# Last batch element of a two-layer graph kernel: s_i and s_j from two-column products right behind the transposes, and the maxima over its first half of keys during its own attention

## The chip, the cores and the metric

The kernel runs on one core of one Trainium2 chip. The metric is the device time of one execution in microseconds, as the median over several runs. A profiled execution gives the times of single instructions; its span runs from the first to the last instruction.

## The reference

Inputs are x (8 batch elements, 2048 nodes, 256 features, float32) and an adjacency matrix of 2048 x 2048. Two layers follow each other:

```python
# layer 0: attention with 4 heads of 64, keys in 8 chunks of 256, a softmax inside each chunk
scores = clip(q @ k.T / 8, -10, 10);  scores = where(mask == 0, -10, scores)
ctx = sum over chunks of softmax(scores in the chunk) @ v in the chunk
h = layernorm(x + (layernorm(ctx @ Wo.T + bo + x) * gamma + beta))
# layer 1: graph attention
Wh = h @ W;  s_i = Wh @ a1;  s_j = Wh @ a2
e = leaky_relu(s_i[:, None] + s_j[None, :], 0.2), -inf where there is no edge
out = layernorm(h + elu(softmax(e) @ Wh))
```

Since the leaky ReLU rises monotonically, the largest e of a query is leaky_relu(s_i + the largest s_j among its neighbours). Layer 1 subtracts it before the exponential, so it needs, for each query, a maximum over all neighbouring keys.

## The kernel before

**Beats.** The nodes are cut into 4 query blocks of 512 (`ib`) and 16 key chunks of 128 (`c`). Layer 0 goes through batch elements, blocks and chunks in one program of 512 beats, one key chunk of one block in each: the scores of four heads on TensorE (L899), the cap by the mask on VectorE (two L909), the exponential on ScalarE (L912), and the products with v of the chunk pair before (L928), copied by ScalarE (L936, L942). Sums of a pair go through two small DMAs and a reciprocal (dc, L950, rd, r), and VectorE and GpSimd scale and add them (L963, L964). Even beats carry the dc and rd DMAs. Batch element 7, the last, has beats 448 to 511. Then come beats without layer 0, here called the tail.

**The order of the work is written out by hand.** Each engine executes its instructions in the order in which the program issues them, and so does SP, the queue that issues all DMAs. Generators are advanced one step per beat in `end_beat`: before beat 512 those of `ahead`, then those of `fins`; from beat 512 on the other way round. A step waits on its engine if its input isn't there, and everything behind it on that engine waits too.

**fin(b, ib)** ends layer 0 for a block: output products (`po`, L357), adds, statistics (L316, L317), a power on GpSimd (L322), scaling on ScalarE (L329), gamma and beta, statistics and scaling once more, the store of h, and eight transposes of h (L383) that ScalarE copies into `hT` (L384). `hT` is stored to DRAM, except that of the last block of batch element 7. Each stage is a step of its own beat. For block (7,3), fin's steps lie in the tail, the transposes in beat 520.

**Layer 1** runs one batch element behind, in steps of one key chunk: ScalarE's L714, VectorE's L718 (with s_j as a scalar) and L723 (the mask), the exponential L727, sums on GpSimd (L734, L736), products with Wh (L746, for the last batch element L761). In the tail one step starts per beat: at its beginning the last block of batch element 6, (6,3), remains, then come the four blocks of batch element 7.

**prelude(b)** prepares layer 1 of batch elements 0 to 6: it loads hT, multiplies it with `W_aug` (L398; 258 columns, that is W with W·a1 and W·a2 as two more), takes the columns s_j, 0.2 s_j and s_i out of `wh` into `sj` (`key_columns`, L408 to L410), transposes s_j and sends it through DRAM to a row on all partitions (`key_rows`, L416 to L421), and then goes over all queries: `half_max` (L438) adds the row to a half row of `far`, which is 0 at edges and hugely negative elsewhere, and keeps the maximum. Half rows come through the two buffers `fb`, loaded by SP (L430) as they get free. `less_max` (L453 to L457) and `query_rows` make what layer 1 needs for a block (`ab`).

**last_prelude(7)** does this for batch element 7. In beats 500, 504 and 508 it loads hT of blocks 0 to 2, and two beats after each it computes `wh` of the block, in the place of kT, which attention has read by then, and its columns of `sj`. From beat 511 it takes the maxima over the first half of the keys (16 of them, `half(it, 0)`), one per beat up to beat 512 and two after. In beat 514 it issues loads of the second half rows of `far`, 4 MB, into eight buffers. When hT of block (7,3) is there it computes `wh` and `sj` of that block and the second row, and takes the maxima over the second half.

Matmul results of all these helpers share two PSUM buffers, tag "m" in the pool `ps_m`; a helper's matmul waits until the buffer's last reader is through.

Of the kernel before, what the change touches and what calls it, by code (L numbers as in the profile page):

```python
# [9 lines left out]
F32 = mybir.dt.float32  # L10
# [9 lines left out]
P = 128  # L20
CLIP = 10.0
EPS = 1e-5
SLOPE = 0.2
# [5 lines left out]
def tile_adj_attention__then__gat(  # L29
# [35 lines left out]
    nc = tc.nc  # L65
    B, N, F = x.shape
    H, D = 4, 64
    CHUNK = 256
    KC = F // P
    NT = N // P  # L70
    IB = 512
    NIB = N // IB
    TPB = IB // P
# [4 lines left out]
    HN = N // 2  # L78
# [259 lines left out]
    fin_near = [0] * B  # L338
# [3 lines left out]
    def fin(b, ib, ctxT):  # L342


        xt = one.tile([P, TPB, F], F32, tag="x", name=f"x{b}_{ib}")
        nc.sync.dma_start(out=xt, in_=x[b, ts(ib, IB), :].rearrange("(t p) f -> p t f", p=P))
        yield
        y = one.tile([P, TPB, F], F32, tag="y", name=f"y{b}_{ib}")
        nc.gpsimd.tensor_add(y, xt, bc_rows(bo_bc))  # L349
        nc.gpsimd.tensor_add(xt, xt, bc_rows(beta_bc))  # L350
        while (b, ib) not in ctx_done or ctx_done[b, ib] == beat:
            yield
        for t2 in range(TPB // 2):
            po = ps_m.tile([P, 2, F], F32, tag="m", name=f"po{b}_{ib}_{t2}")
            for j in range(2):
                for k in range(KC):
                    nc.tensor.matmul(  # L357
                        po[:, j, :],
                        ctxT[:, k, ts(2 * t2 + j, P)],
                        WT["o"][:, k, :],  # L360
                        start=(k == 0),
                        stop=(k == KC - 1),
                    )
            nc.vector.tensor_add(y[:, ts(t2, 2), :], po, y[:, ts(t2, 2), :])
        mv, rstd = yield from stats(y, f"a{b}_{ib}")
        yield
        normalize(y, mv, rstd, f"a{b}_{ib}")
        yield
        engine = nc.vector if (b, ib) == (B - 1, NIB - 1) else nc.gpsimd
        engine.tensor_mul(y, y, bc_rows(gamma_bc))  # L370
        engine.tensor_add(y, y, xt)
        yield
        mv, rstd = yield from stats(y, f"b{b}_{ib}")
        yield
        normalize(y, mv, rstd, f"b{b}_{ib}")
        nc.sync.dma_start(out=h_d[b, ib], in_=y)
        fin_near[b] += 1
        yield
        hT = four.tile([P, KC, IB], F32, tag="xT", name=f"hT{b}_{ib}")
        for k in range(KC):  # L380
            pt = ps_m.tile([P, TPB, P], F32, tag="m", name=f"pt{b}_{ib}_{k}")
            for t in range(TPB):
                nc.tensor.transpose(pt[:, t, :], y[:, t, ts(k, P)], ident)  # L383
            nc.scalar.copy(hT[:, k, :], pt.rearrange("p t c -> p (t c)"))  # L384
        if (b, ib) == (B - 1, NIB - 1):
            states[b]["hT"] = hT
        else:
            nc.sync.dma_start(out=hT_d[b, ib], in_=hT)
# [12 lines left out]
    def load_hT(b, ib):  # L401
        t = four.tile([P, KC, IB], F32, tag="xT", name=f"hTl{b}_{ib}")
        nc.sync.dma_start(out=t, in_=hT_d[b, ib])
        return t

    def key_columns(wh, sj, r):

        nc.vector.tensor_copy(sj[:, 0, r], wh[:, :, F + 1])  # L408
        nc.vector.tensor_scalar_mul(sj[:, 1, r], wh[:, :, F + 1], SLOPE)
        nc.vector.tensor_copy(sj[:, 2, r], wh[:, :, F])  # L410

    def key_rows(b, sj, row, r):

# [61 lines left out]
    def prelude(b):  # L475


        st = states[b]
        while fin_near[b] < NIB:
            yield  # L480
        hts = [load_hT(b, ib) for ib in range(2)]
        yield
        yield
        while blocks_done < b * NIB:
            yield
        wh = one.tile([P, NT, F + 2], F32, tag="wh", name=f"wh{b}")
        for ib in range(NIB):
            wh_block(b, wh[:, ts(ib, TPB), :], hts[ib], ib)
            if len(hts) < NIB:
                hts.append(load_hT(b, len(hts)))  # L490
            yield
        sj = two.tile([P, 3, NT], F32, tag="sj", name=f"sj{b}")
        key_columns(wh, sj, slice(0, NT))
        yield
        sj_row = one.tile([P, N], F32, tag="sj_row", name=f"sj_row{b}")
        key_rows(b, sj, sj_row, slice(0, NT))
        st["wh"], st["sj"] = [wh[:, ts(ib, TPB), :] for ib in range(NIB)], sj
        fbs, fb_load = far_loads(b, [(it, hf) for it in range(NT) for hf in range(2)])
        yield
        yield  # L500
        for ib in range(NIB):
            m2 = two.tile([P, 2, TPB], F32, tag="m2", name=f"m2{b}_{ib}")
            for n in range(2 * TPB):
                half_max(sj_row[:, ts(n % 2, HN)], fbs.pop(0), m2[:, n % 2, n // 2 : n // 2 + 1])
                fb_load()
                if ib or n % 2:
                    yield
            less_max(sj, ib, m2, f"{b}_{ib}")
            yield
            ab_d = query_rows(m2, f"{b}_{ib}")  # L510
            yield

            while blocks_done < b * NIB + ib - 1:
                yield
            st["ab"][ib] = (beat + 2, query_bc(ab_d, f"{b}_{ib}"))

    def last_prelude(b):

        st = states[b]
        wh, rows = [None] * NIB, [None] * 2
        halves = [slice(0, HT), slice(HT, NT)]
        sj = None
        for ib in range(NIB - 1):

            while fin_near[b] <= ib or beat < 2 * total - 12 + 4 * ib:
                yield
            ht = load_hT(b, ib)
            yield  # L530
            yield
            wh[ib] = one.tile([P, TPB, F + 2], F32, tag=f"kT{ib}", name=f"wh{b}_{ib}")
            wh_block(b, wh[ib], ht, ib)
            if sj is None:
                sj = two.tile([P, 3, NT], F32, tag="sj", name=f"sj{b}")
            key_columns(wh[ib], sj, slice(ib * TPB, (ib + 1) * TPB))
            nc.vector.memset(wh[ib][:, :, F : F + 1], 1.0)
            yield
            if ib == 1:
                rows[0] = one.tile([P, HN], F32, tag="v0", name=f"sj_row{b}_0")  # L540
                key_rows(b, sj, rows[0], halves[0])
                fbs, fb_load = far_loads(b, [(it, 0) for it in range(NT)])
        m2 = one.tile([P, NIB, 2, TPB], F32, tag="m2l", name=f"m2{b}")
        firsts = list(range(NT))
        held = None

        def half(it, hf):
            fb = fbs.pop(0) if hf == 0 else held[it // 2][:, ts(it % 2, HN)]
            half_max(rows[hf], fb, m2[:, it // TPB, hf, it % TPB : it % TPB + 1])
            if hf == 0:  # L550
                fb_load()

        while "hT" not in st:
            for it in firsts[: 2 if beat > 2 * total else 1]:
                half(it, 0)
                firsts.remove(it)

            if beat >= 2 * total + 2 and held is None:
                held = []
                for n in range(HT):  # L560
                    fr = eight.tile([P, 2, HN], BF16, tag="e", name=f"far{b}_{n}")
                    nc.sync.dma_start(out=fr, in_=far[2 * n : 2 * n + 2, 1].rearrange("t p w -> p t w"))
                    held.append(fr.rearrange("p t w -> p (t w)"))
            yield
        wh[-1] = one.tile([P, TPB, F + 2], F32, tag=f"kT{NIB - 1}", name=f"wh{b}_{NIB - 1}")
        wh_block(b, wh[-1], st["hT"], NIB - 1)
        key_columns(wh[-1], sj, slice(NT - TPB, NT))
        nc.vector.memset(wh[-1][:, :, F : F + 1], 1.0)
        rows[1] = one.tile([P, HN], F32, tag="v1", name=f"sj_row{b}_1")
        key_rows(b, sj, rows[1], halves[1])  # L570
        st["wh"], st["sj"] = wh, sj
        yield
        while firsts:
            half(firsts.pop(0), 0)
        for ib in range(NIB):
            for t in range(TPB):
                half(ib * TPB + t, 1)
                if ib:
                    yield
            less_max(sj, ib, m2[:, ib], f"{b}_{ib}")  # L580
            ab_d = query_rows(m2[:, ib], f"{b}_{ib}")
            yield

            while blocks_done < b * NIB + ib - 1:
                yield
            st["ab"][ib] = (beat + 1, query_bc(ab_d, f"{b}_{ib}"))
# [213 lines left out]

    l1 = layer1()
    l1_live = True
    ahead = [prelude(b) for b in range(B - 1)] + [last_prelude(B - 1)]
    lows, edged, weighted = [], [], []
    agenda = {}
    beat = 0
# [228 lines left out]
```

## Time and profile before

| | us |
|---|---|
| median of 3 runs | 4392.35 |
| lowest and highest run | 4391.38, 4404.53 |
| the profiled execution, its own time | 4387.29 |
| its span, first to last instruction | 4385.5 |
| TensorE (PE) busy | 4064.2 (93%) |
| VectorE (DVE) busy | 3417.7 (78%) |
| ScalarE (ACT) busy | 2564.4 (58%) |
| GpSimd (POOL) busy | 1760.5 (40%) |

In the profile, PE is TensorE's matmuls and PEld its weight loads. A float32 matmul call appears as several instructions. The number in square brackets at the end of a row of the timeline is the engine's idle time ahead of it, and what released it. The chain view follows the work that ended last back from the end: at each step to what released it, or to the instruction before it on its engine.

### The profile page before, as it was taken

How to read it: one execution, taken by the hardware profiler on the slowest of the kernel's cores; microseconds unless marked ns; L12 is line 12 of the kernel's file. 1: busy time of each engine (PE TensorE's matmuls, PEld its weight loads, DVE VectorE, ACT ScalarE, POOL GpSimd, SP SyncE). 2: the span in 40 equal slices, each digit the busy share in tenths (PEclk: the TensorE clock that was granted, in tenths of full speed). 3: DMA queues.
4: the chain of work that ended last, by engine and by line, in shares of the span. 5: the costliest groups of instructions: out<-in, count | busy, mean ns of one | idle time of the engine just before them, and what ended most of it. 6: DMA issues, size and time to landing. Idle time of an engine off the chain costs nothing. (4 is left out here: it accounts for less than half of the span.)

```text
span 4385.5 us, 61171 instructions
## 1 busy us (share of the span) xinstructions
PE 4064.2 (93%) x23053; PEld 1907.6 (43%) x23053; DVE 3417.7 (78%) x4530; ACT 2564.4 (58%) x3842; POOL 1760.5 (40%) x901
## 2 busy tenths in 40 slices
PE   8889989999999999999899999999999999899767
PEld 3223334454344534454344543445434454344456
DVE  5876589965998669976699766996579965888777
ACT  5655556665566556666566665566556665555546
POOL 0222235543455334444245442554325542354420
PEclk9999999999999999999999999999999999999889
DMA  5554232222332233321333223232232222322321
GB/s 166 182 163 149 71 115 86 83 73 89 99 90 81 64 107 102 100 75 51 105 102 98 74 74 105 85 95 78 70 106 85 89 78 67 115 83 80 123 73 58
DMA packets 257641, 415.63 MB, mean 95 GB/s; under 512 B 85440, under 2 KB 120512, under 8 KB 256448
## 3 DMA queue, kind: packets, MB, share of 16 engines
q1 hardware_dynamic: 257344, 411.71, 30.5%
q8 instruction: 181, 2.97, 0.3%
q14 instruction: 116, 0.95, 0.1%
HBM read 340.66 MB, written 68.88 MB: 93 GB/s over the span
## 5 line engine op out<-in xcount | busy, mean ns | idle before, releaser
L912 ACT ACTIVATE e<-sc 128x1024 f32<-128x1024 f32 x1024 | 1034.2, 1020 | 1049.9 <-DVE sc L909 1006.7
L909 DVE SCALAR_TENSOR_TENSOR sc<-sc,mk 128x1024 f32<-128x1024 f32 x1024 | 1206.7, 1223 | 538.3 <-PE sc L899 352.6
L899 PE MATMUL sc<-qT,kT 64*128 64x512 f32 x4096 | 1060.4, 633 | 86.7 <-ACT e L912 86.2
L964 POOL TENSOR_TENSOR ctxT<-ctxT,un 128x1024 f32<-128x1024 f32 x224 | 568.5, 2538 | 1145.3 <-DVE un L963 1007.0
L928 PE MATMUL u<-e,v 128*32 128x512 f32 x8192 | 980.9, 597 | 0.0
L746 PE MATMUL us<-wh,w 128*128 128x256 f32 x3584 | 878.6, 395 | 81.9 <-ACT w L727 60.4
L746 PEld LDWEIGHTS us<-wh,w 128*128 128x128 f32 x3584 | 667.7, 193 | 422.2 <-ACT w L727 110.7
L736 POOL TENSOR_TENSOR acc<-acc,w 128x512 f32<-128x512 f32 x392 | 601.7, 1535 | 544.9 <-ACT w L727 534.4
L899 PEld LDWEIGHTS sc<-qT,kT 64*128 64x128 f32 x4096 | 347.2, 189 | 611.6 <-ACT e L912 281.8
L718 DVE SCALAR_TENSOR_TENSOR w<-ab,sj,w 128x512 f32<-128x512 f32 x512 | 571.5, 1137 | 4.6 <-ACT w L714 4.5
L928 PEld LDWEIGHTS u<-e,v 128*32 128x32 f32 x8192 | 240.6, 110 | 659.7 <-issue 543.9
L928 PE MATMUL u<-e,ones 128*32 128x512 f32 x4096 | 497.5, 604 | 0.0
L723 DVE TENSOR_TENSOR w<-w,mk 128x512 f32<-128x512 f32 x512 | 458.6, 917 | 37.1 <-DMA mk<-mask 34.6
L438 DVE CUSTOM_DVE_ANT_0 fb<-sj_row,fb 128x1024 bf16<-128x1024 f32 x240 | 387.8, 1626 | 2.3 <-DMA fb<-far 2.3
L714 ACT ACTIVATE w<-ab,sj 128x512 f32<-128x512 f32 x512 | 352.2, 714 | 8.7 <-POOL acc L734 5.4
L727 ACT ACTIVATE w<-w 128x512 f32<-128x512 f32 x512 | 308.8, 629 | 75.9 <-DVE w L723 75.3
L936 ACT COPY un<-u 128x512 f32<-128x512 f32 x512 | 300.5, 587 | 66.5 <-PE u L928 57.6
L963 DVE TENSOR_TENSOR un<-un,r 128x1024 f32<-128x1024 f32 x224 | 278.1, 1242 | 42.2 <-DMA r<-rd 36.7
L928 PEld LDWEIGHTS u<-e,ones 128*32 128x32 f32 x4096 | 107.8, 110 | 356.5 <-issue 305.4
L950 DVE RECIPROCAL dc<-dc 128x16 f32<-128x16 f32 x256 | 63.9, 249 | 149.8 <-DMA dc<-ds 134.0
L942 ACT COPY ds<-u 128x512 f32<-128x512 f32 x256 | 148.5, 580 | 3.0 <-PE u L928 2.5
L349 POOL TENSOR_TENSOR y<-x,bo_bc 128x1024 f32<-128x1024 f32 x32 | 77.6, 2426 | 163.6 <-DMA x<-in_x_dram 103.0
(112 smaller groups left out, 3114.7 us busy)
## 6 DMA issues: line engine op xcount, KB each, us to landing
r<-rd SPq DMA_DIRECT2D x256, 256.0 KB
mk<-mask SPq DMA_DIRECT2D x120, 512.0 KB
fb<-far SPq DMA_DIRECT2D x240, 256.0 KB
xT_k<-in_xT_dram SPq DMA_DIRECT2D x32, 512.0 KB
raw<-in_adjT_dram SPq DMA_DIRECT2D x32, 512.0 KB
rawf<-in_adj_dram SPq DMA_DIRECT2D x32, 512.0 KB
x<-in_x_dram SPq DMA_DIRECT2D x32, 512.0 KB
h_d<-y SPq DMA_DIRECT2D x32, 512.0 KB
```

The costliest lines, as they stand in the source:

```text
L438: nc.vector.tensor_tensor_reduce(out=fb, in0=row, in1=fb, scale=1.0, scalar=2 * FAR * 0.999, op0=ALU.add, op1=ALU.max, accum_out=dst,)
L714: nc.scalar.activation(self.w, k["ab"][:, 1, :], AF.Identity, bias=k["sj"][:, 1, c : c + 1])
L718: nc.vector.scalar_tensor_tensor(self.w, k["ab"][:, 0, :], k["sj"][:, 0, c : c + 1], self.w, ALU.add, ALU.max)
L723: nc.vector.tensor_tensor(self.w, self.w, self.k["mks"][self.c // HT][:, self.c % HT, :], ALU.min)
L727: nc.scalar.activation(self.w, self.w, AF.Exp)
L736: nc.gpsimd.tensor_add(k["acc"], k["acc"], self.w)
L746: nc.tensor.matmul(k["us"][:, t, :], self.w[:, ts(t, P)], k["wh"][c // TPB][:, c % TPB, 0:F], start=(first and t % 2 == 0), stop=last, ski ...
L899: nc.tensor.matmul(sc[:, h, :], kTs[b][c // TPB][h * D : (h + 1) * D, hp, ts(c % TPB, P)], qT[h * D : (h + 1) * D, hp, :], start=True, sto ...
L909: nc.vector.scalar_tensor_tensor(scs[hp], scs[hp], -CLIP, cap, ALU.max, ALU.min)
L912: nc.scalar.activation(e, scs[hp], AF.Exp)
L928: nc.tensor.matmul(m[h * DH : (h + 1) * DH, :], prev["v"][pc // TPB][:, pc % TPB, f0 : f0 + DH] if part < 2 else ones[:, 0:DH], prev["es"] ...
L964: nc.gpsimd.tensor_add(p["ctxT"], p["ctxT"], p["un"])
```

## The change

For batch element 7, s_i and s_j no longer come out of `wh`. In each of its four `fin`, right behind the transposes, a new helper multiplies `hT` with the two extra columns of `W_aug` alone and writes `sj` from PSUM. `last_prelude` is split into two generators. `last_maxima` makes the row of the first half of the keys and takes the first-half maxima as soon as prelude(6) has taken its last maximum and two blocks of key sums are there; it takes two in odd beats and one in even beats. `last_wh` computes `wh` in the beats in which it was computed before. Both half rows now lie in the tile `sj_row`. In beat 520, `last_maxima` comes before `last_wh`.

```diff
@@ fin
             nc.scalar.copy(hT[:, k, :], pt.rearrange("p t c -> p (t c)"))
+        if b == B - 1:
+            key_sums(b, ib, hT)
@@
+    def key_sums(b, ib, hT):
+        st = states[b]
+        if ib == 0:
+            st["sj"] = two.tile([P, 3, NT], F32, tag="sj", name=f"sj{b}")
+        ps = ps_m.tile([P, TPB, 2], F32, tag="m", name=f"ps{b}_{ib}")
+        for t in range(TPB):
+            for k in range(KC):
+                nc.tensor.matmul(
+                    ps[:, t, :], hT[:, k, ts(t, P)], W_aug[:, k, F : F + 2], start=(k == 0), stop=(k == KC - 1)
+                )
+        r = slice(ib * TPB, (ib + 1) * TPB)
+        nc.vector.tensor_copy(st["sj"][:, 0, r], ps[:, :, 1])
+        nc.vector.tensor_scalar_mul(st["sj"][:, 1, r], ps[:, :, 1], SLOPE)
+        nc.vector.tensor_copy(st["sj"][:, 2, r], ps[:, :, 0])
+        st["blocks"] = ib + 1
@@ prelude
             less_max(sj, ib, m2, f"{b}_{ib}")
+            if ib == NIB - 1:
+                st["maxima"] = True
@@ last_prelude becomes last_wh ...
-        for ib in range(NIB - 1):
-            while fin_near[b] <= ib or beat < 2 * total - 12 + 4 * ib:
+        for ib in range(NIB):
+            if ib < NIB - 1:
+                while fin_near[b] <= ib or beat < 2 * total - 12 + 4 * ib:
+                    yield
+                ht = load_hT(b, ib)
                 yield
-            ht = load_hT(b, ib)
-            yield
-            yield
+                yield
+            else:
+                while "hT" not in st:
+                    yield
+                ht = st["hT"]
             wh[ib] = one.tile([P, TPB, F + 2], F32, tag=f"kT{ib}", name=f"wh{b}_{ib}")
             wh_block(b, wh[ib], ht, ib)
-            key_columns(wh[ib], sj, slice(ib * TPB, (ib + 1) * TPB))
             nc.vector.memset(wh[ib][:, :, F : F + 1], 1.0)
             yield
@@ ... and last_maxima
-            if ib == 1:
-                rows[0] = one.tile([P, HN], F32, tag="v0", name=f"sj_row{b}_0")
-                key_rows(b, sj, rows[0], halves[0])
-                fbs, fb_load = far_loads(b, [(it, 0) for it in range(NT)])
+        while "maxima" not in states[b - 1] or st.get("blocks", 0) < 2:
+            yield
+        sj = st["sj"]
+        sj_row = one.tile([P, N], F32, tag="sj_row", name=f"sj_row{b}")
+        key_rows(b, sj, sj_row[:, 0:HN], halves[0])
+        fbs, fb_load = far_loads(b, [(it, 0) for it in range(NT)])
+        yield
+        yield
...
         while "hT" not in st:
-            for it in firsts[: 2 if beat > 2 * total else 1]:
+            for it in firsts[: 1 + beat % 2]:
                 half(it, 0)
                 firsts.remove(it)
...
-        wh_block(b, wh[-1], st["hT"], NIB - 1)
-        key_columns(wh[-1], sj, slice(NT - TPB, NT))
-        key_rows(b, sj, rows[1], halves[1])
+        key_rows(b, sj, sj_row[:, HN:N], halves[1])
@@
-    ahead = [prelude(b) for b in range(B - 1)] + [last_prelude(B - 1)]
+    ahead = [prelude(b) for b in range(B - 1)] + [last_maxima(B - 1), last_wh(B - 1)]
```

More of the change, by code (lines that the diff above doesn't have):

```diff
@@ L515, in prelude, with last_wh, last_maxima @@
             st["ab"][ib] = (beat + 2, query_bc(ab_d, f"{b}_{ib}"))
-    def last_prelude(b):
+    def last_wh(b):
         st = states[b]
-        wh, rows = [None] * NIB, [None] * 2
-        halves = [slice(0, HT), slice(HT, NT)]
-        sj = None
-        for ib in range(NIB - 1):
-            while fin_near[b] <= ib or beat < 2 * total - 12 + 4 * ib:
-                yield
-            ht = load_hT(b, ib)
-            yield
-            yield
+        wh = st["wh"] = [None] * NIB
+        for ib in range(NIB):
[3 more added lines that the diff above has]
+                ht = load_hT(b, ib)
+                yield
+                yield
[3 more added lines that the diff above has]
+                ht = st["hT"]
             wh[ib] = one.tile([P, TPB, F + 2], F32, tag=f"kT{ib}", name=f"wh{b}_{ib}")
             wh_block(b, wh[ib], ht, ib)
-            if sj is None:
-                sj = two.tile([P, 3, NT], F32, tag="sj", name=f"sj{b}")
-            key_columns(wh[ib], sj, slice(ib * TPB, (ib + 1) * TPB))
             nc.vector.memset(wh[ib][:, :, F : F + 1], 1.0)
             yield
-            if ib == 1:
-                rows[0] = one.tile([P, HN], F32, tag="v0", name=f"sj_row{b}_0")
-                key_rows(b, sj, rows[0], halves[0])
-                fbs, fb_load = far_loads(b, [(it, 0) for it in range(NT)])
+    def last_maxima(b):
+        st = states[b]
+        halves = [slice(0, HT), slice(HT, NT)]
+        while "maxima" not in states[b - 1] or st.get("blocks", 0) < 2:
[6 more added lines that the diff above has]
+        yield
         m2 = one.tile([P, NIB, 2, TPB], F32, tag="m2l", name=f"m2{b}")
@@ L548, in half @@
             fb = fbs.pop(0) if hf == 0 else held[it // 2][:, ts(it % 2, HN)]
-            half_max(rows[hf], fb, m2[:, it // TPB, hf, it % TPB : it % TPB + 1])
+            half_max(sj_row[:, ts(hf, HN)], fb, m2[:, it // TPB, hf, it % TPB : it % TPB + 1])
             if hf == 0:
@@ L564, in last_prelude @@
             yield
-        wh[-1] = one.tile([P, TPB, F + 2], F32, tag=f"kT{NIB - 1}", name=f"wh{b}_{NIB - 1}")
-        wh_block(b, wh[-1], st["hT"], NIB - 1)
-        key_columns(wh[-1], sj, slice(NT - TPB, NT))
-        nc.vector.memset(wh[-1][:, :, F : F + 1], 1.0)
-        rows[1] = one.tile([P, HN], F32, tag="v1", name=f"sj_row{b}_1")
-        key_rows(b, sj, rows[1], halves[1])
-        st["wh"], st["sj"] = wh, sj
+        key_rows(b, sj, sj_row[:, HN:N], halves[1])
         yield
```

## The prediction

> **What bounds the kernel now.** I read the page first: busy time per engine, then busy tenths in 40 slices of 109.6 us.
>
> ```profile
> span 4385.5 us, 61171 instructions
> ...
> PE 4064.2 (93%) x23053; PEld 1907.6 (43%) x23053; DVE 3417.7 (78%) x4530; ACT 2564.4 (58%) x3842; POOL 1760.5 (40%) x901
> ...
> PE   8889989999999999999899999999999999899767
> ```
>
> TensorE is nearly full until the last three slices. So the change puts work into a stage that PE fills and takes some out of one where it doesn't. The windows view prices the stages (start:end, length, then PE, weight load, DVE, ACT and POOL busy, granted clock, DMA share, GB/s).
>
> ```profile
> 3924.00:4005.00 81.00, 77.57 (x453) 34.67 (x452) 77.69 (x89) 48.45 (x73) 45.69 (x23) 1.00 0.29 83
> 4005.00:4062.00 57.00, 49.65 (x278) 25.61 (x278) 44.08 (x76) 36.16 (x60) 27.78 (x15) 0.97 0.24 72
> 4062.00:4112.00 50.00, 50.00 (x297) 24.93 (x297) 30.68 (x44) 29.89 (x48) 16.41 (x10) 1.00 0.20 68
> 4112.00:4186.00 74.00, 42.73 (x177) 29.91 (x170) 68.51 (x94) 26.30 (x44) 40.20 (x20) 0.73 0.49 157
> ```
>
> I number beats by DVE's two L909 in each; the last pair, around 4112, is beat 511. Row 4 is beats 512 to 520, up to the last block's transposes: DVE is busy 68.5 of 74 us, PE only 42.7, at clock 0.73. The chain view of 4118 to 4200 says with what (start, us, what):
>
> ```profile
> 4122.31 2.65 DVE fb L438
> 4124.99 6.85 DMA fb<-far
> 4139.01 3.29 DVE fb L438
> 4142.30 3.29 DVE fb L438
> 4155.95 4.68 DMA fb<-far
> ```
>
> First-half maxima (L438 on fb) hold 22.5% of that chain (18.5 us), their loads 14.1% (11.5 us). They stand in DVE's order between the steps of fin(7,3).
>
> **What the skill says.** "GPSIMD Engine Reference", 1. Specifications: GpSimd shares SBUF interfaces with DVE instructions that have two SBUF inputs. The trace agrees: L718 takes 0.66 us alone, 2.83 beside POOL's L349. "TensorE: Matmul & The Clock Gate", What's actually happening: half clock after an idle window of about 3.4 us. It agrees: eight L746 products take 3.78 us after 4.16 idle, 1.99 otherwise.
>
> **The change, part by part.**
>
> *Key sums of blocks (7,0), (7,1), (7,2): beats 472, 488, 504.* Each is 8 matmul calls, 16 instructions of two columns. The nearest row is L597, whose 8 instructions of one column take 0.95 to 1.02 us: I take 2.1 us, between 1.9 (twice 0.95) and 3.65 (L398's 16 of 258 columns). First PE waits for ACT's second hT copy, where today it goes straight on to the next scores, as the timeline of beat 504 shows:
>
> ```profile
> 4059.78 1.06 PE L383 MATMUL pt<-ident,y 128*128 128x128 f32 x8 [0.47 <-ACT ds L942]
> 4060.44 1.07 ACT L384 COPY hT<-pt 128x512 f32<-128x512 f32 x2 [0.33 <-PE pt L383]
> 4060.77 1.99 PE L899 MATMUL sc<-qT,kT 64*128 64x512 f32 x8
> 4061.60 0.25 DVE L950 RECIPROCAL dc<-dc 128x16 f32<-128x16 f32 x1 [4.71 <-DMA dc<-ds]
> ```
>
> Copies end 4061.5, sums 4063.6: the scores of 505 start 2.8 late. On DVE the three column writes (0.17 each, as L408 to L410) wait for the sums, and behind them stand L963 (1.22, now done in the 4.71 us wait), L950 and L718, for which the score cap L909 waits: from 4062.3 to 4065.9, 3.3 us beyond its scores' need at most. Beat 472: 2.7 by the same working (copies end 3789.3, scores now start 3788.6). Beat 488: 2.4, since L597 already waits 0.33 for the copy. Sum **8.4 us**, both engines being nearly full there; no later wait absorbs it, since the 5.0 us wait for a mask at 3802 hangs on the reciprocal that shifts too. POOL's L964 comes later with L963, and idles before it anyway (11.7 us at 4111); the hT store on SP isn't touched. The sums hold one ps_m buffer until the column writes, and its next taker is the part-0 product of the next even beat, 4 us later. Bounds 6 to 14.
>
> *Key rows moved from beat 507 to 499.* prelude(6) ends its maxima in beat 499 (its last L453 group, 4008.1). The transpose (0.27) then stands before fin(7,2)'s output products and takes one of two ps_m buffers; both products wait for ACT copies, the first from 4006.3 to 4009.0. I put 1.9 us on PE less 0.3 saved in 507: **1.6 us**. On SP the row's two DMAs and two fb loads now precede hr (L591), used at 4032: no cost, but 5 us late if the row DMA stalls. Where they leave, at 4085, nothing waited.
>
> *Sixteen first-half maxima in beats 501 to 511, two in odd beats, one in even.* Two, one, two... gives 15 by beat 510 and one in 511, where one stands today. Fifteen come in, 1.14 to 3.3 us each; the fifteen fb loads on SP follow them, and no dc or rd goes out in odd beats, so dc's chain isn't held; 256 KB each into 68 to 72 GB/s is cheap. Even beats: 502, 506, 510 put theirs into DVE's waits for wh copies, 504 and 508 into waits for dc (4.71, 1.75): nothing. Without those waits it is 1.2 each, 6 us. Odd: 501 puts two before L605, with DVE full until L909 of 502 (4032.9), so 2.3 us; 503 puts two before L327, for which ACT's normalisation waits, and behind that PE's next transposes: 2.3. In 505, 507, 509 L909 has 1.1 to 1.4 us of waiting for scores and PE 1.9 us or more before it needs the exponentials: nothing, 2.3 each without. Sum **4.6 us**, bounds 0 to 22 (ten at 2.2, the length beside POOL, all exposed).
>
> The column writes leave beats 502, 506, 510, but the memset of the ones column waits for the same wh copies: no gain.
>
> *The tail, beats 512 to 520.* The number of beats stays: L1 takes one step each, 16 of block (6,3) and then 64, and isn't held by ab. What shrinks is fin(7,3)'s way:
> - To y's end (4150.1). Without the 2.73 at 4122, L599 comes at 4127.4; without the two behind it and their load, L963 at 4131.5, not 4136.7. But PE's 24 products (7.56 us, cold) stand before the output products, start when ACT is through (4131.2, not 4134.5) and so give 3.2; without the halves that delay y's adds to 4148.8, they follow the output products at once: 4143.0. Gain 7.1.
> - To L327 (4159.4): st_a, st_c, one L718 and L723, 6.7 us for 9.3. Gain 2.5.
> - To L370 (4164.3): ACT's 2.1 us bounds it, 2.4 for 5.0. Gain 2.5.
> - To st_b (4172.4): L370, L371, L718, L723, 5.1 for 8.1. Gain 3.
> - To L327 (4179.4): 2.4 of stats, then POOL's power or L718 and L723: 4.5 for 7.0. Gain 2.5.
>
> From there ACT's normalisation and cold products lead, unchanged. Sum **17.6**; bounds 8 (PE products and ACT become the way) to 26 (the chain's 30 less what lies under the loads).
>
> *Last block.* Today hT copies, 3.8 us of wh products, a copy, then the columns at 4191.8. Then: copies, 2.1 us of sums, columns at 4190.1. But the wh products now run while the row's DMAs fly, and their memset holds L718 and L723 ahead of the second halves until 4196.2, where the row lands at 4195.9. Gain **1.3**, bounds 0 to 1.7. All that follows shifts with it.
>
> *Sum.* 8.4 + 1.6 + 4.6 = 14.6 added, 18.9 removed: 4.3 us less. The profiled span of 4385.5 (own time 4387.29) becomes 4381.2. The median of the runs is 4392.35, 5.1 above the profiled execution; I move the median: **4388**.
>
> **The rivals.**
> 1. *The main stage absorbs the additions.* PE was idle 7.4 us in 4005 to 4062[...], which speaks for it; 50.00 of 50.00 in the next row speaks against. Main cost 8 instead of 14.6, tail 25: about 4375.
> 2. *The tail finds another bound.* PE's products at half clock and ACT's release of them (L727) hold each beat, as at 4134.5. Against: these waits are themselves released by DVE's L723, which sits behind the maxima. Tail 9, main 14.6: about 4398, no gain.
> 3. *Slower: DVE becomes the bound of beats 501 to 510.* With one maximum per beat it was already busy 77.7 of 81 us. If each of the ten in odd beats costs 2.2 us in full, that is 22 for 4.6, the sum 32 against a tail of 17: about 4407. It decides from some 32 us of added time on. Against: DVE was busy only 30.7 of 50 where most of them go.
>
> That the change doesn't do what it says, maxima left for the tail, would need prelude(6) to end later than 499; nothing moves it.
>
> **How the numbers follow.** What a measurement can tell from no change is about 0.3%, 13 us: 4379 to 4405.5. Chances: my sum 0.48 (4379 to 4396), rival 1 0.27, rival 2 0.13, rival 3 0.12. Rival 1 is faster, rival 3 slower, the others within: 0.27, 0.61, 0.12. The likeliest's own range is 4379 to 4396; to hold eight in ten it goes down to 4371, most of rival 1, and up to 4401, rival 2.
>
> **What would show it.** Right: no L438 on fb after the first one past 4112; beats 512 to 520 take 53 to 60 us instead of 74; beats 452 to 511 together 10 to 20 us longer, in steps near 472, 488, 499, 501, 503, 504; 16 two-column matmul instructions in about 2.1 us. Wrong: L909 waiting on nothing but DVE's own order through 505 to 510 (rival 3), or L746 cold on every tail beat with DVE idle (rival 2). What I trust least is the delay of PE by the key sums, and which waits near 500 give it back.

## The result, and the profile after

The changed kernel is a little slower. Its median over 22 runs is 4405.11 us (4395.52 to 4412.32), against 4397.34 (4391.38 to 4404.53) for the kernel before in 22 runs beside it: ratio 1.0016 [1.0009, 1.0022]. That is within the 0.3% that the prediction took as the least difference a measurement can tell, and outside the forecast range of 4371 to 4401. Of the 17.1 us between forecast and median, 5.0 are the kernel before, whose median over more runs is 4397.34 instead of 4392.35; 12.1 are the change, forecast at -4.3 and measured at +7.8.

The page of the changed kernel: span, busy time, and the busy tenths of TensorE in 40 slices.

```profile
span 4404.4 us, 61302 instructions
...
PE 4080.4 (93%) x23117; PEld 1918.7 (44%) x23117; DVE 3426.2 (78%) x4530; ACT 2565.1 (58%) x3842; POOL 1757.1 (40%) x901
...
PE   8889989999999999999899999999999999898867
```

The fourth slice from the end, here beats 492 to 503, has fallen from 9 to 8, and that is where time goes. The third has risen from 7 to 8, partly because the tail is better filled and partly because more of the main stage now falls into it. The two profiled spans differ by 18.9 us, but 12.6 of these are there before beat 472, where the programs still do the same; so I compare from beat 472 on. Each stage figure below is read from one profiled execution of its kernel.

I cut both traces at the same instructions: the first cap (L909 before, L932 after) of beats 472, 499, 501, 505 and 511, and the transposes of block (7,3). The windows view of the changed kernel (start:end, length, then PE, weight load, DVE, ACT and POOL busy with the number of instructions, granted clock, DMA share, GB/s; a granted clock of 0.50 means that TensorE ran at half speed):

```profile
3795.50:4019.80 224.30, 210.43 (x1232) 96.28 (x1230) 197.68 (x246) 129.85 (x193) 102.74 (x52) 0.98 0.33 94
4019.80:4040.40 20.60, 17.57 (x93) 10.07 (x95) 12.85 (x29) 10.88 (x19) 3.96 (x3) 0.92 0.35 112
4040.40:4094.20 53.80, 39.72 (x206) 21.62 (x203) 40.41 (x60) 26.68 (x44) 23.30 (x12) 0.89 0.31 94
4094.20:4147.60 53.40, 50.79 (x292) 24.33 (x292) 45.56 (x56) 28.10 (x44) 20.26 (x11) 0.99 0.23 72
4147.60:4203.50 55.90, 38.77 (x184) 27.22 (x177) 47.48 (x65) 26.30 (x44) 37.52 (x20) 0.86 0.43 142
```

Set beside the same cuts of every kernel profiled, in us ("row": from the transposes to the first maximum over the second half of the keys):

| kernel | 472-499 | 499-501 | 501-505 | 505-511 | 511-transposes | row | rest |
|---|---|---|---|---|---|---|---|
| before | 222.2 | 17.1 | 40.1 | 49.3 | 74.3 | 11.6 | 188.0 |
| after | 224.3 | 20.6 | 53.8 | 53.4 | 55.9 | 12.8 | 188.1 |
| e1_sums_only | 224.9 | 17.1 | 42.8 | 50.0 | 73.9 | 12.7 | 188.0 |
| e2_even_only | 225.8 | 20.6 | 44.5 | 49.9 | 65.7 | 13.0 | 188.1 |
| e3_no_first_maxima | 225.9 | 20.4 | 42.8 | 49.9 | 56.3 | 12.9 | 188.1 |
| e4_row_later | 223.9 | 17.2 | 54.3 | 53.0 | 56.1 | 12.7 | 188.0 |
| e5a_no_pool | 224.2 | 17.2 | 47.6 | 53.1 | 55.9 | 12.8 | 188.1 |
| e5b_no_pool_no_maxima | 226.1 | 17.2 | 40.8 | 49.6 | 56.9 | 11.9 | 188.1 |
| e7_spread | 225.0 | 17.2 | 41.5 | 48.9 | 61.0 | 13.0 | 189.4 |
| e6_spread_two_sums | 224.5 | 17.2 | 39.3 | 48.4 | 60.1 | 12.1 | 189.3 |

The tail gives 18.4 us back, as forecast. The main stage, beats 472 to 511, loses 23.3 where 14.6 were forecast, and 13.7 of that lies in four beats, 501 to 504. There the granted clock fell from 0.96 to 0.89, and DVE's busy time rose from 31.54 us to 40.41. The row of these beats in the kernel before:

```profile
4022.20:4062.30 40.10, 34.07 (x192) 16.76 (x188) 31.54 (x48) 25.73 (x43) 23.85 (x13) 0.96 0.24 73
```

What happens in these beats of the changed kernel is in the timeline of 501 and 502 (start, us, engine, line, operation, out<-in; in square brackets the engine's idle time ahead of it and what released it):

```profile
4043.09 1.42 POOL L757 TENSOR_TENSOR acc<-w,w 128x512 f32<-128x512 f32 x1 [9.27 <-ACT w L750]
4043.28 2.32 DVE L457 CUSTOM_DVE_ANT_0 fb<-sj_row,fb 128x1024 bf16<-128x1024 f32 x1
4044.46 3.35 POOL L370 TENSOR_TENSOR y<-y,gamma_bc 128x1024 f32<-128x1024 f32 x1
4045.53 3.37 DVE L457 CUSTOM_DVE_ANT_0 fb<-sj_row,fb 128x1024 bf16<-128x1024 f32 x1
4048.82 3.38 DVE L628 SCALAR_TENSOR_TENSOR hx<-ex,hx 128x1024 f32<-128x1024 f32 x1
4052.13 3.48 DVE L741 SCALAR_TENSOR_TENSOR w<-ab,sj,w 128x512 f32<-128x512 f32 x2
4055.54 2.35 DVE L932 SCALAR_TENSOR_TENSOR sc<-sc,mk 128x1024 f32<-128x1024 f32 x2
4056.79 2.16 ACT L935 ACTIVATE e<-sc 128x1024 f32<-128x1024 f32 x2 [9.12 <-DVE sc L932]
4059.47 6.39 PE L400 MATMUL pw<-W_aug,hTl 128*128 128x258 f32 x16 [6.74 <-ACT ds L965]
```

The two first-half maxima of beat 501 (now L457) run beside GpSimd's sum (L757) and its gamma and beta instructions (L370, L371) and take 2.32 and 3.37 us, and L628 behind them 3.38. These, and two L741 behind them, stand ahead of the cap of beat 502, so ScalarE has been idle 9.12 us when the cap frees its exponential. TensorE has been idle 6.74 us, and the `wh` products then take 6.39 us. In the kernel before, the same 16 take 3.75:

```profile
4036.82 3.75 PE L398 MATMUL pw<-W_aug,hTl 128*128 128x258 f32 x16 [2.28 <-ACT ds L942]
```

The windows view says why they are slow in the changed kernel: the clock is at half during them, and was at 1.00 up to 4058.03.

```profile
4058.04:4064.85 6.81, 5.38 (x13) 4.27 (x14) 2.18 (x4) 2.62 (x5) 0.00 (x0) 0.50 0.13 40
```

Beats 503 and 504 repeat it with another chain:

```profile
4075.85 2.29 DVE L457 CUSTOM_DVE_ANT_0 fb<-sj_row,fb 128x1024 bf16<-128x1024 f32 x1
4078.08 2.29 DVE L457 CUSTOM_DVE_ANT_0 fb<-sj_row,fb 128x1024 bf16<-128x1024 f32 x1
4080.30 0.15 DVE L327 SCALAR_TENSOR_TENSOR nmr_b<-mv_b,rstd_b 128x4 f32<-128x4 f32 x1
4080.48 2.07 ACT L329 ACTIVATE y<-y,nmr_b,rstd_b 128x256 f32<-128x256 f32 x4 [3.73 <-DVE nmr_b L327]
4085.09 3.58 PE L769 MATMUL us<-wh,w 128*128 128x256 f32 x8 [4.07 <-ACT w L750]
4089.89 2.21 PE L422 MATMUL ps<-W_aug,hT 128*128 128x2 f32 x16 [0.24 <-ACT hT L384]
```

ScalarE's normalisation waits for L327 behind two maxima, and the weights w of layer 1 stand behind the normalisation on ScalarE; TensorE idles 4.07 us and does the eight products (L746 before, now L769) in 3.58 us. The last line is a key sum: 16 instructions of two columns in 2.21 us.

### The profile page after: what moved, and what is told of

It is laid out like the page before. It is cut to its first block, busy times and chain, and to the rows that moved or that the text cites. A ratio compares the mean times of both kernels' runs of the same rounds, so it can differ in the third digit from the quotient of the medians.

```text
span 4404.4 us, 61302 instructions
## 1 busy us (share of the span) xinstructions
PE 4080.4 (93%) x23117; PEld 1918.7 (44%) x23117; DVE 3426.2 (78%) x4530; ACT 2565.1 (58%) x3842; POOL 1757.1 (40%) x901
## 5 line engine op out<-in xcount | busy, mean ns | idle before, releaser
L932 DVE SCALAR_TENSOR_TENSOR sc<-sc,mk 128x1024 f32<-128x1024 f32 x1024 | 1206.5, 1222 | 536.1 <-PE sc L922 349.5
L769 PE MATMUL us<-wh,w 128*128 128x256 f32 x3584 | 876.0, 394 | 71.8 <-ACT w L750 50.1
L769 PEld LDWEIGHTS us<-wh,w 128*128 128x128 f32 x3584 | 665.3, 192 | 412.0 <-ACT w L750 101.1
L741 DVE SCALAR_TENSOR_TENSOR w<-ab,sj,w 128x512 f32<-128x512 f32 x512 | 574.9, 1144 | 12.1 <-issue 6.0
L746 DVE TENSOR_TENSOR w<-w,mk 128x512 f32<-128x512 f32 x512 | 460.4, 920 | 37.0 <-DMA mk<-mask 34.4
L457 DVE CUSTOM_DVE_ANT_0 fb<-sj_row,fb 128x1024 bf16<-128x1024 f32 x240 | 390.1, 1635 | 0.0
L959 ACT COPY un<-u 128x512 f32<-128x512 f32 x512 | 300.4, 587 | 64.7 <-PE u L951 55.0
L400 PE MATMUL pw<-W_aug,hTl 128*128 128x258 f32 x496 | 130.2, 414 | 28.1 <-ACT un L959 19.8
```

The costliest lines, as they stand in the source:

```text
L457: nc.vector.tensor_tensor_reduce(out=fb, in0=row, in1=fb, scale=1.0, scalar=2 * FAR * 0.999, op0=ALU.add, op1=ALU.max, accum_out=dst,)
L741: nc.vector.scalar_tensor_tensor(self.w, k["ab"][:, 0, :], k["sj"][:, 0, c : c + 1], self.w, ALU.add, ALU.max)
L746: nc.vector.tensor_tensor(self.w, self.w, self.k["mks"][self.c // HT][:, self.c % HT, :], ALU.min)
L769: nc.tensor.matmul(k["us"][:, t, :], self.w[:, ts(t, P)], k["wh"][c // TPB][:, c % TPB, 0:F], start=(first and t % 2 == 0), stop=last, ski ...
L932: nc.vector.scalar_tensor_tensor(scs[hp], scs[hp], -CLIP, cap, ALU.max, ALU.min)
```

## The experiments

Theory A, after the comparison of the two traces: the maxima in odd beats carry most of the loss, and the sums and the row only some 10 us of it together. The rivals are named in the expectations.

**e1_sums_only: the sums stay, row and maxima return to their old beats.**

```diff
-        while "maxima" not in states[b - 1] or st.get("blocks", 0) < 2:
+        while "maxima" not in states[b - 1] or beat < 2 * total - 5:
...
-        yield
-        yield
+        while beat < 2 * total - 1:
+            yield
...
-            for it in firsts[: 1 + beat % 2]:
+            for it in firsts[: 2 if beat > 2 * total else 1]:
```

> The changed kernel with its key sums, but the key row in beat 507 and the first-half maxima from beat 511, as in the kernel before. The trace of the changed kernel has steps of +2.8, -1.6, +1.9 and +3.6 us at the beats after the key sums. Theory A (the additions to the main stage are mostly the maxima): beats 472 to 511 take 6 to 8 us more than the 328.7 of before, the tail (cap of beat 511 to the transposes) about 74 as before, the way from there to the second-half maxima 11.6 to 12.8; so 7 to 9 us slower than before. Theory B (the sums carry most of the 23.3 us, since PE and DVE stand still for them): 15 to 20 us more in beats 472 to 511, and 16 to 21 us slower than before.

Measured: 4400.74 us (4394.69 to 4409.94) against 4393.83 for the kernel before, ratio 1.0013 [1.0007, 1.0020]. In the table the stages up to 511 grow by 2.7, 0, 2.7 and 0.7: the sums cost 6.1 us, and the tail is as before (73.9). This is near what Theory A expected. The sums alone are thus a loss, and they aren't the cause of the rest. In the 6.1 lies a gain of 0.35 in each of the beats 502, 506 and 510, from which the column writes are gone.

**e2_even_only: two maxima in even beats, none in odd ones.**

```diff
-            for it in firsts[: 1 + beat % 2]:
+            for it in firsts[: 2 if beat >= 2 * total or beat % 2 == 0 else 0]:
```

> The changed kernel with two first-half maxima in even beats and none in odd ones until beat 511; ten are taken in beats 502 to 510, the last six in beats 512 to 514. Theory A (maxima in odd beats are paid, because DVE has no wait there and runs beside GpSimd; in even beats they fill waits): beats 472 to 511 take 10 to 13 us more than before instead of 23.3, the tail 63 to 67 us instead of 55.9; 1 to 6 us faster than the changed kernel. Theory B (sums and row carry the cost): beats 472 to 511 still take 18 us or more longer than before, and the kernel is 3 to 8 us slower than the changed one.

Measured: 4395.69 us (4389.52 to 4408.47), ratio 1.0005 [0.9997, 1.0013]. Beats 501 to 505 take 44.5 us and 505 to 511 take 49.9, against 42.8 and 50.0 with no maxima there (e1). Ten maxima in even beats thus come with 1.6 us, and these lie in one step, from the cap of 502 to that of 503, where the `wh` products take 5.44 us instead of 3.75. TensorE's wait ahead of them is as in the kernel before (2.28 us), and the first maximum of that beat starts 0.6 us after them, so the maxima don't delay them. It is the clock, at half from 4046.91 to 4050.31 in this execution. Six maxima stay for the tail, which takes 65.7. Even beats are as free as forecast; what the change loses is in the odd ones.

**e3_no_first_maxima: the row and the loads as changed, the maxima left out.**

```diff
             for it in firsts[: 1 + beat % 2]:
-                half(it, 0)
+                fbs.pop(0)
+                fb_load()
```

> The changed kernel without the sixteen first-half maxima: their loads stay, the instructions are left out and the maxima stand at 0, so that the softmax of batch element 7 is shifted by another number than in the reference. Theory A: beats 472 to 511 take 9 to 11 us more than before (sums 6 to 7, row in beat 499 3.5), the tail 54 to 56; so 6 to 9 us faster than before and 13 to 16 faster than the changed kernel. Theory B: beats 472 to 511 stay 18 us or more above before, and the whole is within 4 us of the changed kernel.

Measured: 4390.53 us (4378.42 to 4399.63), ratio 0.9989 [0.9981, 0.9997]. Beats 501 to 505 fall from 53.8 to 42.8 us, 505 to 511 from 53.4 to 49.9: the maxima cost 11.0 + 3.5 = **14.5 us** in the beats where they stand. Over the whole stage from 472 to 511 the difference is 13.1, because beats 472 to 499, the same in both programs, took 1.6 more in e3; that stretch spreads from 223.9 to 226.1 among the kernels in which it is the same program, so such differences of 2 us there say nothing. The main stage and the tail are near what Theory A expected, the whole less so: it had 6 to 9 us faster than before, and the medians show 3 to 5 (ratio 0.9989).

**e4_row_later: the row in beat 500 instead of 499.**

```diff
         sj = st["sj"]
+        yield
         sj_row = one.tile([P, N], F32, tag="sj_row", name=f"sj_row{b}")
...
         yield
-        yield
```

> The changed kernel with the key row (transpose, copy, two DMAs, two loads of half rows) one beat later, in beat 500, away from the output products of block (7,2). Theory A (in beat 499 the transpose takes one of two PSUM buffers ahead of those products): the step of 3.5 us at beat 500 goes to 0.5 or less, at most 1.5 comes back in beat 501, and the kernel is 2 to 3.5 us faster than the changed one. Theory B (any beat has the same contention for the buffers): 3 us or more reappear in beat 501, no difference in time. A third outcome: the row lands too late for the maxima of beat 501, DVE waits for it, and the kernel is slower by that wait.

Measured: 4400.43 us (4392.48 to 4406.60), ratio 1.0012 [1.0003, 1.0020]. Beats 499 to 501 take 17.2 us instead of 20.6 (17.1 before): the row's cost in beat 499, 3.5 us, goes away if it comes one beat later. In the timeline, the changed kernel's output products of beat 499:

```profile
4023.85 5.38 PE L357 MATMUL po<-WT_o,ctxT 128*128 128x256 f32 x16 [2.55 <-ACT un L959]
```

Before, the first eight of these started at 4006.30 right behind the products of layer 1, and the 16 took 1.89 and 1.99 us with a gap of 0.85 between. The transpose of the row takes one of the two buffers of `ps_m`, so TensorE waits 2.55 us ahead of the first half until ScalarE has emptied the other (L959). The 16 then take 5.38 us instead of 3.88, because the clock is at half:

```profile
4023.91:4027.31 3.40, 3.40 (x8) 2.74 (x9) 0.00 (x0) 1.98 (x4) 0.00 (x0) 0.50 0.10 20
```

So Theory A holds for the stage. Of its 2 to 3.5 us in the whole time the medians show 1.8 (1.0012 against 1.0016), with intervals that overlap. Something of the third outcome is there too: the first maximum waits 0.91 us for its load.

**e5a_no_pool and e5b_no_pool_no_maxima: e4 without GpSimd's two instructions of block (7,2), with and without the maxima.** This asks how much of the cost in beats 501 to 505 is the sharing with GpSimd (A1) and how much the mere place in DVE's order (A2).

```diff
-        engine.tensor_mul(y, y, bc_rows(gamma_bc))
-        engine.tensor_add(y, y, xt)
+        if (b, ib) != (B - 1, 2):
+            engine.tensor_mul(y, y, bc_rows(gamma_bc))
+            engine.tensor_add(y, y, xt)
```

> The changed kernel with the row in beat 500, and without GpSimd's two instructions on block (7,2) of layer 0 (times gamma, plus the residual with beta), so that h of this block isn't the reference's. It is read against the next kernel, which has no first-half maxima beside that. Theory A1 (the two maxima of beat 501 cost 4.7 us instead of 2.3 since GpSimd works beside them): with GpSimd quiet they last 1.2 us each, and the step from beat 501 to 502 is 2.3 to 2.6 us longer here than in the next kernel. Rival A2 (it is the order on DVE and what waits for it, whoever works beside it): the step stays 4.2 us or more longer.

> The same without the sixteen first-half maxima (their loads stay; the maxima stand at 0, so batch element 7's softmax is shifted by another number). It gives the base for the step at beat 502. Both theories: that step is 4 to 6 us shorter than in the kernel before, because DVE's two L718 and L605 no longer stand beside GpSimd.

Measured, one run each: 4396.03 and 4388.99 us; only their traces are used. With GpSimd's two instructions (e4) beats 501 to 505 take 54.3 us, without them (e5a) 47.6, and without the maxima too (e5b) 40.8. So the maxima cost 6.8 us without those two instructions, and 6.7 us more with them. Of these 6.7, 4.1 lie in the step to the cap of 502 and 2.5 in the next, where the `wh` products take 6.24 us in e4 (at half clock, after 6.62 us of idling) and 3.75 in e5a. What e4 would take without its maxima wasn't run, and e1 and e3 (42.8) aren't its base: with the row in beat 500 and no maxima in 501, the step to 502 is 2.2 us shorter than before, with GpSimd's two instructions (e6, e7) as without them (e5b). The last section says why. The 4 to 6 us that both theories had for that step in e5b are thus a miss: DVE's two L718 still take 4.57 us there instead of 5.63, since GpSimd's next instructions move up beside them.

In the trace of e5a the maxima of beat 501 and L605 (there L629) run at their own length, although all three still stand ahead of the cap, and the first waits 1.42 us for its load:

```profile
4041.13 1.23 DVE L458 CUSTOM_DVE_ANT_0 fb<-sj_row,fb 128x1024 bf16<-128x1024 f32 x1 [1.42 <-DMA fb<-far]
4042.28 1.22 DVE L458 CUSTOM_DVE_ANT_0 fb<-sj_row,fb 128x1024 bf16<-128x1024 f32 x1
4043.43 1.22 DVE L629 SCALAR_TENSOR_TENSOR hx<-ex,hx 128x1024 f32<-128x1024 f32 x1
```

The step from the cap of 501 to that of 502 is 2.7 us longer in e5a than in e5b, near what A1 expects and below A2. The step from 503 to 504, where GpSimd's pair doesn't run, is 3.4 us longer than before in both e4 and e5a, and unchanged in e5b: that part is the wait of L327 behind two maxima. But they run beside GpSimd's sum there (L760 in e5a) and take 2.29 us each in both kernels. At 1.2 us each the step would have grown by some 2.3, an estimate. So A1 holds for beat 501; in 503 most of the cost is the order, as A2 says, and some 1.1 us is sharing with another of GpSimd's instructions. TensorE's clock has no part in it up to there: in e5a it stays at 1.00 from the cap of 501 to 4075.10, in beat 504.

**e7_spread: row in beat 500, and maxima only where DVE waits anyway.** None in 501 and 503, two in 502, 504, 506 and 510, one in the others.

```diff
         sj = st["sj"]
+        yield
...
-            for it in firsts[: 1 + beat % 2]:
+            due = {501: 0, 502: 2, 503: 0, 504: 2, 506: 2, 510: 2}.get(beat, 1)
+            for it in firsts[:due]:
```

> The changed kernel with the row in beat 500 and the first-half maxima put where DVE has waits: two in beats 502, 504, 506, 510, one in 505, 507, 508, 509, 511, none in 501 and 503, and the last three one each in beats 512 to 514. Key sums as in the change. Theory A: beats 472 to 511 take 7 to 9 us more than before (sums 6.1 to 6.7, maxima 1 to 2.5), the tail 59 to 62 us, the way to the second-half maxima 12.7: 3 to 5 us faster than before. Rival (any maximum in beats 505 to 511 is paid in full): beats 472 to 511 take 13 us or more, and the kernel is level with before or slower.

Measured: 4392.25 us (4374.90 to 4396.86) against 4397.85 for the kernel before in that comparison, ratio 0.9985 [0.9978, 0.9991], some 6 us faster where Theory A had 3 to 5. Beats 472 to 511 take 3.9 us more than before, where it had 7 to 9. Thirteen maxima now lie in beats 502 to 511, and beats 501 to 511 take 90.4 us, less than the 92.8 of e1 without any; 2.2 of that is a gain of another kind, told in the last section, and the thirteen cost about nothing (e5b, which has that gain and no maxima, takes 90.5). Three stay for the tail, 61.0 us. The rest, behind the first maximum over the second half, is 1.4 us longer than before; why wasn't followed up.

**e6_spread_two_sums: as e7, and sums of two columns only for the two blocks that the first row needs.** Their matmuls stand one beat behind the transposes, their column writes in the middle of the beat after (`mids`); blocks (7,2) and (7,3) take their columns out of `wh` as before.

```diff
-        if b == B - 1:
-            key_sums(b, ib, hT)
...
+        if b == B - 1 and ib < 2:
+            yield
+            key_sums(b, ib, hT)
...
+        mids.append(columns)
...
+            if ib >= 2:
+                key_columns(wh[ib], st["sj"], slice(ib * TPB, (ib + 1) * TPB))
             nc.vector.memset(wh[ib][:, :, F : F + 1], 1.0)
```

> The same maxima and row, but two-column sums only for blocks (7,0) and (7,1): their matmuls one beat after the transposes, so that PE need not wait for ScalarE's copy, and their three columns on DVE in the middle of the beat after, so that DVE need not wait for PE. Blocks (7,2) and (7,3) take their columns from wh, as before. Theory A: each sum costs PE's 2.1 us and no more, a part of it given back at the mask wait of beat 475; beats 472 to 511 take 3 to 5.5 us more than before, the tail 59 to 62 us, the way to the second-half maxima 11.6: 7 to 10 us faster than before. Rival (the sums' cost is not their waits but the matmuls and the buffer they hold): 6 us or more for beats 472 to 511, and no more than 5 us faster than before.

Measured: 4386.36 us (4380.89 to 4393.47), ratio 0.9976 [0.9967, 0.9985], some 10 us below the kernel before, as Theory A had it, and the fastest of all. Beats 472 to 511 take 329.4 us, 0.7 more than before, with the same 2.2 in them; 3 to 5.5 were expected. The tail gives 14.2. The row comes 0.5 late and the rest 1.3. What the key sum of (7,2) cost in beat 504 (2.7 and 0.7 in e1) isn't paid, and that is most of the 3.2 us by which this main stage is shorter than e7's. Whether the later places of the other two sums help isn't shown: beats 472 to 499 take 224.5 us here and 225.0 in e7.

## Why the prediction was wrong

The forecast sum against what the runs show, in us:

| term | forecast | measured | from |
|---|---|---|---|
| key sums of three blocks | +8.4 | +6.1 | e1 against before |
| row in beat 499 | +1.6 | +3.5 | beats 499 to 501, after against before |
| first-half maxima in beats 501 to 511 | +4.6 | +14.5 | after against e3 |
| tail, beats 512 to 520 | -17.6 | -18.4 | after against before |
| last block's way to the row | -1.3 | +1.2 | after against before |
| sum | -4.3 | +6.9 | directly +6.3 |

**The step that failed** is "Sixteen first-half maxima in beats 501 to 511", sum 4.6 us. Its order was right: even beats nothing (the 1.6 of e2 are the clock's), 501 and 503 the dear ones. Three things in it were not.
- Beat 501 was priced at 2.3, two instructions of 1.14 to 1.21. The prediction cites the Trainium skill ("GPSIMD Engine Reference", 1. Specifications) on the sharing of SBUF interfaces, but used the length beside GpSimd only in the bounds. Yet L370 and L371 stood in that beat in the trace of before too, where L605 already took 2.33 us instead of 1.22. The step to 502 grew by 4.5. For beat 503, 2.3 were forecast and the step to 504 grew by 3.4, both maxima running at 2.29 us beside GpSimd's sum.
- A late cap isn't over when DVE has caught up. TensorE, idle for 6.74 us, ran the `wh` products of beat 502 in 6.39 us instead of 3.75, and the step to 503 grew by 2.3. Over four kernels that step follows these products: at 3.75 us it is 0.35 below before (e1), at 5.44 it is 1.3 above (e2), at 6.24 2.1 (e4), at 6.39 2.3 (after), each 0.35 below the products' excess. "TensorE: Matmul & The Clock Gate", What's actually happening, speaks of half clock after an idle window; the trace agrees, with a clock of 0.50 from 4058.04 on, behind those 6.74 us. The prediction used this for the tail's products and not for the main stage.
- In 505, 507 and 509 the maxima were to fill waits of the cap for its scores. They overfill them: the steps to 506, 507 and so on up to 511 change by +3.3, -2.4, +3.0, +0.7, +1.8 and -2.4 us, where e3 has +1.0, -0.4, +0.2, 0, 0 and -0.3. Two maxima at up to 2.30 us, beside GpSimd, are more than the wait of 1.1 to 1.4, and the next beats give only part of it back: 3.5 us, for nothing forecast.

So the bound of 22 us, "ten at 2.2, the length beside POOL, all exposed", was the right picture for the odd beats and two thirds of it came true. Rival 3, "DVE becomes the bound of beats 501 to 510", is the closest in kind: from 506 to 510 no cap waits for its scores, the sign it named. But its 32 us of added time came to 23.3, and its 4407 lies near the measured 4405.11 partly because the kernel before sat 5.0 higher than the three runs it was worked from. The main stage is also past the 10 to 20 us that the prediction named as a sign of being right. Rival 3's chance of 0.12 was, as it turned out, too low, and so was the upper end of the range, which stopped at rival 2.

**The key sums** cost less, 6.1 instead of 8.4, and the difference lies in the first two. The eight kernels that are the same from beat 472 to 499 take 1.7 to 3.9 us more there than the kernel before, 2.8 in the mean, where 5.1 were forecast; beat 504 costs 3.4 in e1 with all that follows, near the forecast 3.3, but only because the column writes that leave three beats, "no gain" in the prediction, give back 0.35 us each. For beat 472 "no later wait absorbs it" was wrong. In the changed kernel's trace the wait for a mask that took 5.01 us before is 3.46, and the step to 475 gives back 1.6 of the 2.8 lost by 473: counted from the cap of 472, the reciprocal comes 2.9 us later than before, and the mask's load starts only 1.3 later. The column writes behaved as told: DVE idles 6.94 us in beat 504 until the sums are there.

**The row** was put at 1.9 us of waiting for the lost buffer, and that was right: the first product starts 4.03 us behind the cap of 499 instead of 1.19, which alone would end the 16 some 2.0 us later. The other 1.5 us are the half clock behind that wait, which the step left out.

**The tail** went as reckoned. Measured from the cap of beat 511 on, y's end comes 7.9 us earlier (forecast 7.1), the first L327 11.2 (9.6), the second 18.7 (17.6). Only one maximum of the first half is left past that cap. The forecast window of 53 to 60 us for it holds 55.9. Rival 2, that the tail finds another bound, is out. Rival 1, that the main stage absorbs the additions, holds for e7's and e6's places and not for those of the change.

**The last block's way** failed in one size: the `wh` products behind the sums take 5.41 us, not 3.8, at half clock from 4208.23 to 4211.63. In the timeline of the changed kernel:

```profile
4208.07 5.41 PE L400 MATMUL pw<-W_aug,hT 128*128 128x258 f32 x16
...
4213.94 0.74 DVE L741 SCALAR_TENSOR_TENSOR w<-ab,sj,w 128x512 f32<-128x512 f32 x1 [6.01 <-issue]
...
4216.31 1.21 DVE L457 CUSTOM_DVE_ANT_0 far<-sj_row,far 128x1024 bf16<-128x1024 f32 x1
```

As forecast, the memset holds L741 and L746 ahead of the second half; it now waits for the last `wh` copy, which ends at 4213.89. In the kernel before the maxima wait for the row itself:

```profile
4197.50 1.23 DVE L438 CUSTOM_DVE_ANT_0 far<-sj_row,far 128x1024 bf16<-128x1024 f32 x1 [3.91 <-DMA sj_row<-sj_d]
```

The row was ready earlier relative to the transposes (the first column is written 4.1 us behind them instead of 5.8), and the work put ahead of its user used that up and 1.2 us more. e6, which keeps the old order there, loses 0.5.

Not settled is how often the half clock falls on these products: the stages are read from one execution of each kernel, and e2 shows that the same gap can be paid or not.

## What to carry to other kernels

Work taken off a critical tail is only won if it goes into waits; before placing an instruction, look at what its engine does in that very beat, what stands behind it there, and which other engine's instruction it will run beside, and use the length it has beside that one. An even spread (two here, one there) is no substitute: thirteen maxima, mostly in beats where DVE waited anyway, cost about nothing (e7), the change's fifteen 14.5 us. A gap that this opens on TensorE can be paid twice, as a wait and as half clock behind it. If a small product is needed early for part of the blocks only, make it for those alone.

## What the runs showed of the hardware that was not expected

**Who starts first on the shared side of SBUF.** In the kernel before, GpSimd's sum starts 0.18 us ahead of DVE's L605, and L605 takes almost twice its time:

```profile
4024.90 1.42 POOL L734 TENSOR_TENSOR acc<-w,w 128x512 f32<-128x512 f32 x1 [9.27 <-ACT w L727]
...
4025.08 2.33 DVE L605 SCALAR_TENSOR_TENSOR hx<-ex,hx 128x1024 f32<-128x1024 f32 x1
4027.33 5.63 DVE L718 SCALAR_TENSOR_TENSOR w<-ab,sj,w 128x512 f32<-128x512 f32 x2
```

In e7, where a small copy for the row stands on ScalarE ahead of the sum's input, the same pair starts in the other order, DVE 0.19 us ahead:

```profile
4039.68 1.22 DVE L629 SCALAR_TENSOR_TENSOR hx<-ex,hx 128x1024 f32<-128x1024 f32 x1
...
4039.87 2.19 POOL L758 TENSOR_TENSOR acc<-w,w 128x512 f32<-128x512 f32 x1 [9.76 <-ACT w L751]
4040.82 4.55 DVE L742 SCALAR_TENSOR_TENSOR w<-ab,sj,w 128x512 f32<-128x512 f32 x2
```

DVE keeps 1.22 us and GpSimd pays (2.19 for 1.42). The cap of the next beat comes 2.2 us earlier than in the kernel before. e6 has the same order and the same gain, and so has e5b, where GpSimd has no gamma and beta to do there; e1 and e3 have the order and the step of the kernel before. So a shift of less than 0.4 us between two engines decides over 2.2 us of the path, which wasn't planned. This is read from these six traces; no run was made for it alone.

**The clock after little work.** Not only idle time makes the `wh` products slow. In the last block they follow the 16 two-column products and the row's transpose with gaps under 0.3 us and take 5.41 us, while in the kernel before, straight behind the transposes, they take 3.81. TensorE is busy for 2.85 of the 3.40 us from 4204.81 on, at clock 1.00, and from 4208.23 the clock is at half for 3.40 us. That 3.4 us at half clock cost 1.7 fits the 5.41. The other seven kernels with these sums in the last block show it too (six take 5.40 or 5.41 us, e5b 5.11); in e6, without them, the products take 4.17.

After nearly the same idle time the price differs: 5.44 us in e2 after 2.28 us of idling, 3.75 in e3 after 2.27 and in the kernel before after 2.28. In e2 the clock drops to half under the running products:

```profile
4046.91:4050.31 3.40, 3.40 (x10) 2.65 (x9) 2.06 (x4) 0.75 (x2) 0.00 (x0) 0.50 0.31 107
```

In the other two it stays at 1.00 across them. What decides between the two cases isn't shown by these runs.
